# A graph layer with attention, mixing and experts: the PSUM banks and the places in the step of the chain of maxima

## The chip, the cores and the metric

The kernel runs on one core of a Trainium2 chip. The metric is the device time of one execution in microseconds; before the change it is 8320.49 us, the median of three runs (8315.88 to 8325.9). The core has five engines with a queue of instructions each, worked off in order: TensorE (PE, with its weight loads PEld), VectorE (DVE), ScalarE (ACT), GpSimd (POOL) and SyncE (SP). Results of PE go to PSUM, which here is used as eight banks of 512 float32 per partition.

## The reference

One block works on 6250 nodes of 256 features and 200,000 edges. The input is normalised; then come a graph network of three attention layers, a mixing layer of linear attention, and a mixture of eight experts, each added to the stream. What the change touches is the attention over edges, which for each layer is

```python
xh = (h @ W).reshape(n, heads, d)
a_s = (xh * att_src).sum(-1)
a_d = (xh * att_dst).sum(-1)
alpha = jax.nn.leaky_relu(a_s[src] + a_d[dst], NEG_SLOPE)
amax = jax.ops.segment_max(alpha, dst, num_segments=n)
e = jnp.exp(alpha - amax[dst])
z = jax.ops.segment_sum(e, dst, num_segments=n)
alpha = e / (z[dst] + 1e-16)
out = jax.ops.segment_sum(xh[src] * alpha[:, :, None], dst, num_segments=n)
```

Layers 0 and 1 have four heads, layer 2 has one. Every node also has an edge to itself.

## The kernel before, in words

The edges are ordered by their target. They are cut into rows of 128 edges, one edge on each partition, and each row belongs to one block of 128 target nodes. A **step** s has 32 rows; a layer has 51 steps, with one more for rare inputs. The loop in `sum_messages` runs over the steps, and inside it over 16 **iterations** i. In iteration i of step s the instructions of step s itself (its messages are summed) and of step n = s + 1 (its scores are made) are issued side by side. `Order.keep` fixes the order of the text for every engine, so an instruction's place in the loop is its place in its engine's queue.

What stands in the loop for step s:

- `gather`: POOL issues one indirect DMA for a row (L549), eight to a tile. The pool `rows` has 8, 9 and 7 tiles in layers 0, 1 and 2. A tile's gathers come after i = 3, 7, 11 and 15, when `pair` has read the tile that is to be overwritten.
- `hot` (L572, DVE) makes the matrices of zeros and ones that send an edge's message to its target; `weigh_step` multiplies the rows by the edges' weights, partly on ACT (L717) and partly on DVE (L710, which reads a copy of the weights in PSUM, `w_ps`, two of them in turn).
- `pair` (L747, PE): two rows are multiplied and summed in a bank of the pool `pm` (three banks). `add_up` (L760, DVE) adds the bank to the block's sum `acc` two iterations later; PE's pair i thus waits for DVE's add of pair i - 3.

And for step n:

- `scores` (L583, PE; L587, ACT), for two steps at once, in i = 2 to 6 of every second step.
- `spread` (L599, PE), four rows in each i from 0 to 7, sends the targets' scores to the edges; `load_lanes` (SP) and `compare_lanes` (L564, DVE) prepare it. L793 (DVE, i = 8) sums its three parts to `exs`.
- `row_scores` (L606, ACT, i = 2, 4, 6 and 9) copies the source scores out of the gathered rows to `asc`.
- `maxima`, a generator, makes the running maxima over edges of one target: transpose of asc on PE (L616, end of i = 9), scans on DVE (L620 to L625, top of 10), product on PE (L628, end of 10), scans over the rows (L632 to L641, top of 11), product (L644, end of 11), second scans (L652 to L665, top of 12), transpose back and two small products (L668, L671, L672, end of 12), the weights before exp (L676 to L689, top of 13), exp on ACT (L691, top of 14), copies and the column of maxima (L696, L700, DVE, end of 14).

All PSUM tiles of scores, spread and maxima have the name `sm` in a pool of two banks: a tile takes the bank that is free when its turn comes. Another bank, `lane_ps`, is written by DVE alone: it holds the lanes 0 to 127 and the two `w_ps`. With three banks for `pm` and two for the work beside, all eight are in use.

Beside the steps runs other work in pieces, `beside.step()` at the end of each iteration: the mixing layer in layer 0; and in every layer `Layer.update` for four finished blocks of nodes at a time (weights of the self edge L1450, L1453, norms, the next layer's projection, and in layer 2 the experts L1589 to L1606).

Of the kernel before, what the change touches and what calls it, by code (L numbers as in the profile page):

```python
# [7 lines left out]
F32 = mybir.dt.float32  # L8
# [7 lines left out]
P = 128  # L16
# [466 lines left out]
def sum_messages(tc, pools, consts, q, node_rows, adn, h, acc, beside, begin, slot, last,  # L483
# [92 lines left out]

    def scores(s):


        pt = smp.tile([P, 3 * h, SU], F32, name="sm")  # L580
        for i in range(4):
            for k in range(i * 3 * h // 4, (i + 1) * 3 * h // 4):
                nc.tensor.matmul(pt[:, k, :], adt[:, k // 3, k % 3, :], T[s]["block_hot"],  # L583
                                 start=True, stop=True)
            yield
        A[s] = wk.tile([P, h, 3, SU], BF16, name="adc")
        nc.scalar.copy(A[s].rearrange("p k j c -> p (k j) c"), pt)  # L587
# [5 lines left out]
    def spread(s, c0, n):  # L593

        m = M[s]
        if c0 == 0:
            m["ex"] = smp.tile([P, SU, h, 3], F32, name="sm")
        for c in range(c0, c0 + n):
            nc.tensor.matmul(m["ex"][:, c], lanes[s * subs + c // SUB][:, c % SUB, :],  # L599
                             adc(s)[:, :, :, c // 2], start=True, stop=True)  # L600

    def row_scores(s, k):
        m = M[s]
        if k == 0:
            m["asc"] = wk.tile([P, h, SU], F32, name="asc")
        nc.scalar.copy(m["asc"][:, :, k * SUB:(k + 1) * SUB].rearrange("p h c -> p c h"),  # L606
                       rows[s * subs + k][:, :, body:])

    def maxima(s):

        m, t = M[s], T[s]
        asc, exs = m["asc"], m["exs"]
        run = M[s - 1]["run"] if s else run0[:h]
        cut, joins = t["cut"][:hs], t["joins"]
        at = smp.tile([P, P], F32, name="sm")
# [11 lines left out]
        pe = smp.tile([P, 2, SU], F32, name="sm")  # L627
# [15 lines left out]
        pc = smp.tile([P, 2, SU], F32, name="sm")  # L643
# [3 lines left out]
        nc.vector.tensor_scalar(on[:h, :h], consts["ident"][:h, :h], run, None, op0=OP.mult)  # L647
        u = lp.tile([P, 2, h, SU], F32, name="u")
        nc.vector.tensor_add(u[:, 0], asc, exs)
        yield  # L650
# [16 lines left out]
        mt = m["mt"] = smp.tile([P, h, SU], F32, name="sm")  # L667
        nc.tensor.transpose(mt.rearrange("p h c -> p (h c)"), mx[:hs, :],  # L668
                            consts["ident"][:hs, :hs])
        po = smp.tile([P, 2, HEADS], F32, name="sm")  # L670
        nc.tensor.matmul(po[:, 0, :h], consts["ones"][:h, :], on[:h, :h], start=True, stop=True)  # L671
        nc.tensor.matmul(po[:, 1, :h], consts["ones"][:hs, :], new[:hs, :h], start=True,  # L672
                         stop=True)
        yield

        nc.vector.tensor_tensor(u[:, 1], mt, exs, op=OP.add)  # L676
# [17 lines left out]
        if half:  # L694
            m["w_ps"] = consts["w_ps"][:, s % 2].rearrange("p (h c) -> p h c", h=h)
            nc.vector.tensor_copy(m["w_ps"], w)  # L696
# [80 lines left out]
    for s in range(-1, end):  # L777
# [7 lines left out]
        for i in range(HSU):  # L785

            if made and i in (2, 4, 6, 9):
                row_scores(n, (2, 4, 6, 9).index(i))
            if made and 10 <= i <= 14:
                next(chain)  # L790
            if made and i == 8:
                M[n]["exs"] = wk.tile([P, h, SU], F32, name="exs")
                nc.vector.tensor_reduce(M[n]["exs"].rearrange("p k c -> p c k"), M[n]["ex"],  # L793
                                        axis=AX.X, op=OP.add)
            if s < 0 and i * GRP < NB:
                nc.vector.memset(acc[:, i * GRP:min(NB, (i + 1) * GRP), :], 0.0)
# [12 lines left out]
            if made and i == 9:  # L809
                chain = maxima(n)  # L810
            if made and 9 <= i <= 12 or made and i == 14:
                next(chain, None)

            if made and i < 8:
                spread(n, i * GRP, GRP)
                if i % 2:
                    load_lanes(n * subs + i // 2 + nlanes)
                    if i < 7:
                        compare_lanes(n * subs + i // 2 + 1)
            if made and i == HSU - 1:  # L820
                compare_lanes((n + 1) * subs)
            if 2 <= i <= 6:
                next(ahead, None)
# [399 lines left out]
def graph_block(ctx, tc, i, out):  # L1223
# [66 lines left out]
    for l, h in enumerate(heads):  # L1290
        W = C + 2 * h
        with ExitStack() as lc:
# [6 lines left out]
            ps = pool("lane_ps", 1, space=PS).tile([P, 3, P], F32, name="lane_ps")  # L1299
            consts["lane_ps"] = ps[:, 0]  # L1300
            nc.vector.tensor_copy(consts["lane_ps"], consts["lane"])
            consts["w_ps"] = ps[:, 1:]
            pmp, smp = pool("pm", 3, space=PS), pool("smp", 2, space=PS)
# [50 lines left out]
class Experts:  # L1354
# [26 lines left out]
class Layer:  # L1381
# [26 lines left out]
    def update(self, pools, where, stream, beside=None):  # L1408
# [41 lines left out]
        nc.vector.tensor_tensor(xv, xv, ws[:, 0, :n, :, None].to_broadcast([P, n, h, d]),  # L1450
# [3 lines left out]
                                ws[:, 1, :n, :, None].to_broadcast([P, n, h, d]), op=OP.mult)  # L1454
# [223 lines left out]
```

## Time and profile before

| what | value |
|---|---|
| median of three runs | 8320.49 us |
| the profiled execution | 8415.92 us |
| its span | 8414.1 us |
| mean granted clock of TensorE | 0.794 |
| PE busy | 5892.1 us, 70% |
| VectorE busy | 4682.9 us, 56% |
| ScalarE busy | 3410.1 us, 41% |
| GpSimd busy | 4829.7 us, 57% |
| gathers, L549 | 4896, 981 ns each |
| steps of layer 0 | 266 to 2785 us |
| steps of layer 1 | 2932 to 5367 us |
| steps of layer 2 | 5485 to 8243 us |

The first starts and last starts of L757, which comes once a step, give the three stretches. The profile is one execution; a line such as L628 is a line of the kernel before. In the groups, what stands behind the bar is the time for which the engine was idle just before these instructions, and what released it. "issue" means that nothing in the record ended just before, "remote" that the release was seen but not an instruction of the record that ended with it. The ends of matmuls are modelled.

### The profile page before, as it was taken

Reading aid. Unit: us, or ns where it says so; the run is one execution under the profiler, and the core shown is the slowest. Engines: PE = TensorE matmul, PEld = TensorE weight load, DVE = VectorE, ACT = ScalarE, POOL = GpSimd, SP = SyncE. Lnnn points to the kernel's source line nnn. Section 1 sums busy time; section 2 is a strip of 40 time slices with the busy share of each in tenths; the row PEclk is TensorE's granted clock in tenths of the full one; section 3 lists DMA queues with packets and bytes.
Section 4 is the critical chain, followed back from the end, with each engine's and each line's share of the span. In section 5 each row is a group of like instructions: output and inputs, shape, how many; then the busy total and the mean of one; then the engine's idle time right before and its main releaser. Section 6 shows DMA issues by size and latency. Waiting matters only on the chain. (4 is left out here: it accounts for less than half of the span.)

```text
span 8414.1 us, 98030 instructions
## 1 busy us (share of the span) xinstructions
PE 5892.1 (70%) x24601; PEld 4047.1 (48%) x24601; DVE 4682.9 (56%) x13248; ACT 3410.1 (41%) x10628; POOL 4829.7 (57%) x4942
## 2 busy tenths in 40 slices
PE   4577777766665356555566656458889888898998
PEld 3344455544443234434344444235666656566666
DVE  4456666666665455555556555445445445555552
ACT  2344544444443233433333344224444444444443
POOL 3565656565666466666666666456555555555550
PEclk8787877776767677776666776668999999999999
DMA  5444444444444344444444444334444444554452
GB/s 163 118 134 124 132 119 131 117 127 128 136 124 117 83 116 120 122 126 121 116 122 132 121 119 128 91 103 142 144 140 143 142 134 137 146 147 140 148 149 84
DMA packets 616289, 1070.08 MB, mean 127 GB/s; under 512 B 193175, under 2 KB 348167, under 8 KB 615706
## 3 DMA queue, kind: packets, MB, share of 16 engines
q0 software_dynamic: 236672, 661.50, 28.3%
q1 hardware_dynamic: 370590, 389.03, 15.3%
q10 hardware_dynamic: 8444, 13.02, 0.4%
q8 instruction: 214, 3.51, 0.2%
q14 instruction: 369, 3.02, 0.1%
HBM read 1008.69 MB, written 56.03 MB: 127 GB/s over the span
## 5 line engine op out<-in xcount | busy, mean ns | idle before, releaser
L549 POOL DMA_INDIRECT g<-node_rows,src_t x4896 | 4800.6, 981 | 3292.7 <-issue 1366.5
L747 PE MATMUL pm<-g,hot 128*128 128x264 f32 (+1 forms) x9792 | 3376.0, 482 | 1271.0 <-issue 584.3
L747 PEld LDWEIGHTS pm<-g,hot 128*128 128x128 f32 x9792 | 2148.3, 235 | 2020.3 <-issue 864.8
L717 ACT ACTIVATE g<-g,w 128x65 f32<-128x65 f32 (+1 forms) x8160 | 2382.6, 370 | 207.0 <-issue 191.9
L760 DVE TENSOR_TENSOR acc<-acc,pm 128x264 f32 (+1 forms) x2448 | 1030.5, 421 | 687.5 <-remote 278.3
L572 DVE TENSOR_TENSOR hot<-lane_ps,lane_t 128x1024 f32<-128x1024 f32 x612 | 744.2, 1216 | 0.0
L710 DVE TENSOR_TENSOR g<-g,lane_ps 128x520 f32<-128x520 f32 x816 | 559.5, 686 | 32.8 <-issue 31.0
L691 ACT ACTIVATE w<-w 128x128 f32<-128x128 f32 (+1 forms) x153 | 43.2, 282 | 1139.4 <-DVE u L456 500.4
L599 PEld LDWEIGHTS <-hot_t 128*128 128x128 bf16 x4896 | 323.0, 103 | 345.6 <-issue 146.4
L1594 ACT ACTIVATE moe_h<-fa,moe_b 128x512 f32<-128x512 f32 (+1 forms) x208 | 137.8, 662 | 758.8 <-PE fa L1589 460.5
L1589 PE MATMUL fa<-et,moe_w 128*128 128x512 f32 (+1 forms) x832 | 412.3, 621 | 45.3 <-DVE eo L1606 24.5
L1601 PE MATMUL fa<-moe_w,moe_h 128*128 128x256 f32 x1600 | 396.8, 390 | 36.7 <-ACT moe_h L1594 25.5
L1601 PE MATMUL fk<-moe_w,moe_h 128*128 128x256 f32 x1536 | 383.0, 393 | 26.5 <-DVE eo L1606 23.9
L1589 PE MATMUL fk<-et,moe_w 128*128 128x512 f32 (+1 forms) x832 | 384.5, 585 | 18.0 <-ACT moe_h L1594 10.2
L599 PE MATMUL sm<-adc,hot_t 128*128 128x12 bf16 (+1 forms) x4896 | 329.1, 179 | 74.0 <-issue 59.5
L793 DVE TENSOR_REDUCE exs<-sm 128x128 f32<-128x384 f32 (+1 forms) x153 | 69.4, 454 | 546.4 <-remote 386.0
L1601 PEld LDWEIGHTS fa<-moe_w,moe_h 128*128 128x128 f32 x1600 | 294.1, 191 | 90.6 <-ACT moe_h L1594 36.1
L1601 PEld LDWEIGHTS fk<-moe_w,moe_h 128*128 128x128 f32 x1536 | 289.9, 195 | 72.1 <-DVE eo L1606 27.8
L628 PE MATMUL sm<-ends,hcol 128*4 128x64 f32 (+1 forms) x306 | 47.8, 246 | 393.9 <-DVE ends L625 186.1
L1606 DVE SCALAR_TENSOR_TENSOR eo<-fa,share,eo 128x256 f32<-128x256 f32 x200 | 96.1, 481 | 408.6 <-PE fa L1601 239.5
L564 DVE TENSOR_SCALAR hot_t<-hot_t,pidx 128x1024 bf16<-128x1024 bf16 x612 | 299.3, 489 | 41.5 <-DMA hot_t<-q_lane_rows 34.9
L620 DVE TENSOR_TENSOR_SCAN mx_f<-cut_t,sm 128x128 f32<-128x128 bf16 (+1 forms) x153 | 63.2, 413 | 333.8 <-remote 250.7
(385 smaller groups left out, 5827.5 us busy)
## 6 DMA issues: line engine op xcount, KB each, us to landing
hot_t<-q_lane_rows SPq DMA_DIRECT2D x612, 256.0 KB
moe_w<-in_L_ffn_W_dram SPq DMA_DIRECT2D x208, 512.0 KB
g<-node_rows,src_t POOLq DMA_INDIRECT x4896
ea<-node_rows SPq DMA_DIRECT2D x24, 528.0 KB
et<-xnt SPq DMA_DIRECT2D x24, 512.0 KB
hid<-eo SPq DMA_DIRECT2D x24, 512.0 KB
eold<-hid SPq DMA_DIRECT2D x24, 512.0 KB
node_rows<-r ACTq DMA_DIRECT2D x12, 528.0 KB
```

What stands on the lines that cost most here:

```text
L549: nc.gpsimd.indirect_dma_start(out=t[:, c, :], out_offset=None, in_=node_rows, in_offset=bass.IndirectOffsetOnAxis(ap=T[s]["src"][:, i:i + ...
L564: nc.vector.tensor_scalar(lanes[m], lanes[m], consts["pidx"], None, op0=OP.is_equal)
L572: nc.vector.tensor_tensor(t, consts["lane_ps"][:, None, :].to_broadcast([P, SUB, P]), T[s]["lane"][:, k * SUB:(k + 1) * SUB, None].to_broa ...
L599: nc.tensor.matmul(m["ex"][:, c], lanes[s * subs + c // SUB][:, c % SUB, :], adc(s)[:, :, :, c // 2], start=True, stop=True)
L710: nc.vector.tensor_tensor(x, x, w[:, :, c:c + n].rearrange("p h c -> p c h")[:, :, :, None].to_broadcast([P, n, h, d1]), op=OP.mult)
L717: nc.scalar.activation(x, x, AF.Copy, scale=w[:, j, c + i:c + i + 1])
L747: nc.tensor.matmul(pm, m["hots"][2 * i // SUB][:, k + j, :], t[:, k + j, :], start=(j == 0), stop=(j == 1))
L760: nc.vector.tensor_tensor(at, at, pm, op=OP.add)
L1589: nc.tensor.matmul(pt[:, :w], w1[:, k, j * P:(j + 1) * P], xt[:, k, :w], start=(k == 0), stop=(k == 1))
L1594: nc.scalar.activation(hx[:, j, :w], pt[:, :w], AF.Gelu, bias=self.b1[:, e * 4 + j:e * 4 + j + 1])
L1601: nc.tensor.matmul(pt[:, :C], hx[:, j, t * P:(t + 1) * P], w2[:, j, :], start=(j == 0), stop=(j == 3))
L1606: nc.vector.scalar_tensor_tensor(y[:, t, :], pt[:, :C], share[:, t, e:e + 1], y[:, t, :], op0=OP.mult, op1=OP.add)
```

## The change

The pool of two banks becomes one bank with the name `sm` and one with the name `ex`. `spread` has `ex` for itself. `scores` takes the whole of `sm`, and `maxima` takes it once a step and lays its five results side by side in it. The places of the instructions in the step change with it, and the table gives them (top: before the iteration's weights and adds; end: after its pair).

| what | before | after |
|---|---|---|
| scores | i = 2 to 6 | i = 1 to 5 |
| row_scores | 2, 4, 6, 9 | 2, 4, 5, 7 |
| spread | 0 to 7, four each | 0 to 8, four, from i = 5 three |
| load_lanes | 1, 3, 5, 7 | 1, 3, 6, 8 |
| sum of spread (exs) | top of 8 | top of 11 |
| transpose of asc | end of 9 | end of 7 |
| first scans | top of 10 | end of 8 |
| product of the ends | end of 10 | top of 9 |
| scans over the rows | top of 11 | top of 10 |
| product back | end of 11 | end of 10 |
| second scans | top of 12 | end of 11 |
| transpose back, small products | end of 12, transpose first | top of 12, transpose last |
| weights, exp, copies | 13, 14, 14 | 13, 14, 14 |

`w_ps` becomes a single copy. `exs` is copied to the bank `lane_ps` for the first of its two sums. The weights of the self edge are written to that bank too and read from there.

```diff
+    def bank():
+        return smp.tile([P, 512], F32, name="sm")
...
-        pt = smp.tile([P, 3 * h, SU], F32, name="sm")
+        pt = bank()[:, :3 * hs].rearrange("p (k c) -> p k c", k=3 * h)
...
-            m["ex"] = smp.tile([P, SU, h, 3], F32, name="sm")
+            m["ex"] = smp.tile([P, SU, h, 3], F32, name="ex")
...
-        at = smp.tile([P, P], F32, name="sm")
+        sm = bank()
+        at = sm[:, :P]
...
-        pe = smp.tile([P, 2, SU], F32, name="sm")
+        pe = sm[:, P:P + 2 * SU].rearrange("p (k c) -> p k c", k=2)
...
-        pc = smp.tile([P, 2, SU], F32, name="sm")
+        pc = sm[:, P + 2 * SU:P + 4 * SU].rearrange("p (k c) -> p k c", k=2)
...
+        yield
         u = lp.tile([P, 2, h, SU], F32, name="u")
-        nc.vector.tensor_add(u[:, 0], asc, exs)
-        yield
+        exs_ps = consts["exs_ps"][:, :hs].rearrange("p (h c) -> p h c", h=h)
+        nc.vector.tensor_copy(exs_ps, m["exs"])
+        nc.vector.tensor_add(u[:, 0], asc, exs_ps)
...
-        mt = m["mt"] = smp.tile([P, h, SU], F32, name="sm")
-        nc.tensor.transpose(mt.rearrange("p h c -> p (h c)"), mx[:hs, :],
-                            consts["ident"][:hs, :hs])
-        po = smp.tile([P, 2, HEADS], F32, name="sm")
+        k = P + 4 * SU
+        po = sm[:, k + hs:k + hs + 2 * HEADS].rearrange("p (k h) -> p k h", k=2)
...
+        nc.tensor.transpose(sm[:, k:k + hs], mx[:hs, :], consts["ident"][:hs, :hs])
+        mt = m["mt"] = sm[:, k:k + hs].rearrange("p (h c) -> p h c", h=h)
...
-            if made and i in (2, 4, 6, 9):
-                row_scores(n, (2, 4, 6, 9).index(i))
-            if made and 10 <= i <= 14:
-                next(chain)
-            if made and i == 8:
+            if made and i in (2, 4, 5, 7):
+                row_scores(n, (2, 4, 5, 7).index(i))
+            if made and i == 11:
...
+            if made and i in (9, 10, 12, 13, 14):
+                next(chain)
...
-            if made and i == 9:
+            if made and i == 7:
                 chain = maxima(n)
-            if made and 9 <= i <= 12 or made and i == 14:
+            if made and i in (7, 8, 10, 11, 14):
                 next(chain, None)
...
-            if made and i < 8:
-                spread(n, i * GRP, GRP)
+            if made and i < 9:
+                spread(n, 4 * i - max(0, i - 5), 4 - i // 5)
...
-            if 2 <= i <= 6:
+            if 1 <= i <= 5:
                 next(ahead, None)
...
-            ps = pool("lane_ps", 1, space=PS).tile([P, 3, P], F32, name="lane_ps")
+            ps = pool("lane_ps", 1, space=PS).tile([P, 4, P], F32, name="lane_ps")
...
-            pmp, smp = pool("pm", 3, space=PS), pool("smp", 2, space=PS)
+            pmp, smp = pool("pm", 3, space=PS), pool("smp", 1, space=PS)
...
+        wp = consts["own_ps"][:, :2 * GRP * h].rearrange("p (k n h) -> p k n h", k=2, h=h)
         for k in range(2):
-            nc.vector.tensor_mul(ws[:, k, :n], ws[:, k, :n], rz[:, :n])
+            nc.vector.tensor_mul(wp[:, k, :n], ws[:, k, :n], rz[:, :n])
```

More of the change, by code (lines that the diff above doesn't have):

```diff
@@ L611, in maxima @@
         m, t = M[s], T[s]
-        asc, exs = m["asc"], m["exs"]
+        asc = m["asc"]
         run = M[s - 1]["run"] if s else run0[:h]
         cut, joins = t["cut"][:hs], t["joins"]
-        at = smp.tile([P, P], F32, name="sm")
+        sm = bank()
+        at = sm[:, :P]
         nc.tensor.transpose(at[:hs, :], asc.rearrange("p h c -> p (h c)"), consts["ident"])
@@ L673, in maxima @@
                          stop=True)
+        nc.tensor.transpose(sm[:, k:k + hs], mx[:hs, :], consts["ident"][:hs, :hs])
+        mt = m["mt"] = sm[:, k:k + hs].rearrange("p (h c) -> p h c", h=h)
         yield
-        nc.vector.tensor_tensor(u[:, 1], mt, exs, op=OP.add)
+        nc.vector.tensor_tensor(u[:, 1], mt, m["exs"], op=OP.add)
         leaky(nc, u, u)
@@ L694, in maxima @@
         if half:
-            m["w_ps"] = consts["w_ps"][:, s % 2].rearrange("p (h c) -> p h c", h=h)
+            m["w_ps"] = consts["w_ps"].rearrange("p (h c) -> p h c", h=h)
             nc.vector.tensor_copy(m["w_ps"], w)
@@ L808, in sum_messages @@
                 blocks(s + k // subs, k % subs) if s >= 0 or k == subs else None
-            if made and i == 9:
+            if made and i == 7:
                 chain = maxima(n)
-            if made and 9 <= i <= 12 or made and i == 14:
+            if made and i in (7, 8, 10, 11, 14):
                 next(chain, None)
-            if made and i < 8:
-                spread(n, i * GRP, GRP)
[L816 to L819, printed above, removed]
+            if made and i < 9:
+                spread(n, 4 * i - max(0, i - 5), 4 - i // 5)
+                if i in (1, 3, 6, 8):
+                    load_lanes(n * subs + (1, 3, 6, 8).index(i) + nlanes)
+                if i in (1, 3, 5):
+                    compare_lanes(n * subs + i // 2 + 1)
             if made and i == HSU - 1:
                 compare_lanes((n + 1) * subs)
-            if 2 <= i <= 6:
+            if 1 <= i <= 5:
                 next(ahead, None)
@@ L1298, in graph_block @@
             lp, gp, wk = pool("lay", 1), pool("rows", (8, 9, 7)[l]), pool("scores", 2)
-            ps = pool("lane_ps", 1, space=PS).tile([P, 3, P], F32, name="lane_ps")
-            consts["lane_ps"] = ps[:, 0]
+            ps = pool("lane_ps", 1, space=PS).tile([P, 4, P], F32, name="lane_ps")
+            consts["lane_ps"], consts["w_ps"], consts["exs_ps"] = [ps[:, k] for k in range(3)]
+            consts["own_ps"] = ps[:, 3, :2 * GRP * HEADS]
             nc.vector.tensor_copy(consts["lane_ps"], consts["lane"])
-            consts["w_ps"] = ps[:, 1:]
-            pmp, smp = pool("pm", 3, space=PS), pool("smp", 2, space=PS)
+            pmp, smp = pool("pm", 3, space=PS), pool("smp", 1, space=PS)
             ew, es, eps_ = pool("nodes", 1), pool("nodes_sm", 2), pool("nodes_ps", 1, space=PS)
@@ L1449, in update @@
         xv = x[:, :n, :body].rearrange("p n (h d) -> p n h d", h=h)[:, :, :, :d]
-        nc.vector.tensor_tensor(xv, xv, ws[:, 0, :n, :, None].to_broadcast([P, n, h, d]),
+        nc.vector.tensor_tensor(xv, xv, wp[:, 0, :n, :, None].to_broadcast([P, n, h, d]),
                                 op=OP.mult)
@@ L1453, in update @@
         nc.vector.tensor_tensor(ov, acc[:, :, :, :d],
-                                ws[:, 1, :n, :, None].to_broadcast([P, n, h, d]), op=OP.mult)
+                                wp[:, 1, :n, :, None].to_broadcast([P, n, h, d]), op=OP.mult)
         yield
```

## The prediction, made before the changed kernel was run

> **What bounds the kernel now.** I read the busy time by stretch first, with the stretches cut at the three layers (columns: stretch, length, busy time of PE, PE weight loads, DVE, ACT, POOL, granted TensorE clock, DMA share, GB/s).
>
> ```profile
> 266.00:2785.00 2519.00, 1755.10 (x7274) 1184.03 (x7273) 1622.77 (x4501) 1146.87 (x4060) 1535.41 (x1568) 0.77 0.44 125
> 2932.00:5367.00 2435.00, 1460.19 (x5890) 1002.86 (x5889) 1392.89 (x3752) 937.68 (x3661) 1533.99 (x1560) 0.71 0.43 120
> 5485.00:8243.00 2758.00, 2367.86 (x10077) 1640.73 (x10077) 1418.69 (x4235) 1182.94 (x2545) 1547.49 (x1576) 0.91 0.47 139
> ```
>
> Each row is one layer of 51 steps: layers 0, 1, 2. In layers 0 and 1 nothing is above 70%; PE is at 70 and 60%, at a clock of 0.77 and 0.71. In layer 2 PE is at 86% and 0.91: that layer is PE's. A step takes 2519/50 = 50.4, 48.7 and 55.2 us.
>
> Next, POOL in layer 1 (groups by line within the layer; after the bar: busy, mean ns, idle before and what ended it).
>
> ```profile
> L549 POOL DMA_INDIRECT g<-node_rows,src_t x1560 | 1534.0, 983 | 892.7 <-issue 412.6 <-PE pm L747 213.6 <-remote 122.4
> ```
>
> A gather takes 0.98 us and the timeline shows 0.305 us between two that wait for nothing: 32 x 1.288 = 41.2 us a step. This is the floor of layers 0 and 1; the rest of POOL's idle time waits for row buffers that PE has not given back. So PE and DVE, waiting for each other, set 50.4 and 48.7.
>
> Where they wait: PE's and DVE's groups of layer 1.
>
> ```profile
> L747 PE MATMUL pm<-g,hot 128*128 128x264 f32 x3206 | 1243.2, 532 | 696.8 <-issue 282.0 <-DVE acc L760 203.6 <-ACT g L717 104.2
> L628 PE MATMUL sm<-ends,hcol 128*4 128x64 f32 x100 | 16.6, 260 | 150.9 <-DVE ends L625 69.9 <-DVE mx_b L621 40.2 <-DVE ends L624 24.8
> L644 PE MATMUL sm<-cf,hrow 4*128 4x64 f32 x100 | 26.9, 358 | 21.9 <-DVE cf L641 13.3 <-DVE rb L636 3.0 <-PE pm L747 2.6
> L668 PE MATMUL sm<-ident,mx_b 128*128 128x128 f32 x50 | 20.1, 401 | 57.7 <-DVE mx_b L660 53.2 <-DVE mx_f L657 4.6
> ...
> L793 DVE TENSOR_REDUCE exs<-sm 128x128 f32<-128x384 f32 x50 | 27.9, 559 | 283.3 <-remote 260.6 <-PE pm L747 20.3 <-PE sm L599 2.3
> ```
>
> The chain of maxima (i = 9 to 14 of a step's 16 iterations) goes from PE to DVE and back four times, each answer wanted half an iteration later. L793 (i = 8) needs the spread matmuls that PE issued just before. "remote" there means that DVE was released well after the record has the matmul ended: PE is late by its own, and more freedom doesn't cure that part.
>
> The starts of L747 in the timeline, sorted by place in the step, give PE's idle time ahead of pair i in layers 0, 1 and 2: pair 9: 73, 189, 38; pair 14: 67, 167, 6 us. Pair 9 needs a bank that add L760 of pair 6 frees, and that add stands behind L793 on DVE. Pair 14 needs the add behind L676 to L689. In layer 1, pairs 8 to 14 take 26.3 us of a step, and the nine others 21.7.
>
> **The change, part by part.**
>
> *Banks and places.* The chain's idle time on PE, summed over the layers: pair 9 (held by L793) 300; L628 89.8 + 150.9 + 59.2 = 300; L644 66.6 + 21.9 + 38.6 = 127; pair 14 240: 967 us. After the change L793 is at i = 11 where spread ends at i = 8 (from one boundary to over two iterations); the transpose is at the end of i = 7 and its scans at the end of i = 8; L628 at the top of 9, its readers at the top of 10; L644 at the end of 10, its reader at the end of 11; the transpose back (L668) at the top of 12, its reader at the top of 13. Each round trip gains about one iteration (3 us). Against it: PE now has less lead where L628 and L668 wait (an iteration's top instead of its end), and L668 stands behind the two small products, 0.87 us later by the timeline. I take half of the 967 as PE's own lateness, and two thirds of the other half as gone: -320 us (ends: 0 and -880. The latter is what pairs 8 to 14 cost above the pace of the nine others: 4.9, 9.4 and 3.3 us a step in the three layers, times 50). L668's own 131 us stay; +20 for its lost lead (0 to +60).
>
> *One bank against a rule.* The transposes and products of the chain share a bank, and the Trainium skill, PSUM — Partial Sum Buffer, PSUM bank collisions raise a hardware error, wants accesses guarded by bank and quadrant, not by address: each PE write would wait for any DVE read of the bank. Four writes a step, each behind a scan (L657: 476 ns), would be 4 x 153 x 0.476 = 291 us. But in this chain each PE write takes what DVE computed after its last read of the bank, so the wait is there already (the row of L668 ends on mx_b, the scan itself); only scores, at i = 1, must wait for L700 at i = 14 before. I take 0.
>
> *row_scores from 9 to 7.* The fourth copy L606 now heads ACT's i = 7 and the transpose on PE follows it.
>
> ```profile
> L606 ACT COPY asc<-g 128x8 f32<-128x8 f32 x199 | 38.7, 194 | 103.3 <-DMA g<-node_rows,src_t 102.8
> ```
>
> This is layer 2: ACT there already waits for rows at the old place. The rows pool has 7 tiles in layer 2, so this tile's gathers are released by pair 3 of the same step, take 8 x 1.255 = 10 us on POOL, and land 1.9 us after the last issue (the shortest waits of L606). From the last gather's end to pair 7 the layer has a median of 1.0 us (lower quarter -1.0), to pair 9, 7.8. Landing plus a 0.2 us copy against the end of pair 7, step by step: PE would wait 1.8 us on average, 51 x 1.8 = +92 us on the engine that bounds the layer. Layers 0 and 1 (8 and 9 tiles) have 9.7 and 19.4 us: nothing. Below: 0, if PE is late anyway; above: +200, if ACT, held in order, also brings L717 and the gelu L1594 late (2 us more a step).
>
> *exs to PSUM.* One copy a step more, nearest row L696 (288 ns with four heads): 153 x 0.29 = +44 us on DVE, ahead of pick on its queue, where the matmul of the end of i = 10 is awaited anyway; exposed for a third: +15 (0 to +44). own_w written to PSUM: 78 small products of another destination, 0.
>
> *POOL's port.* By the Trainium skill, SBUF — State Buffer, Who interferes with whom, a DVE operation with two SBUF inputs blocks a GpSimd one that reads SBUF for its whole length: 78 x 1.16 (L1450, L1453) + 153 x 0.244 (L649) = 128 us of POOL would come free. The page infers that descriptor generation is not stopped so. The trace lies between: of all 4896 gathers (median 949 ns) what is above 945 ns and lies most beside L1450, L1453 and L649 sums to 11 + 8 + 2: 20 us. And POOL is not the bound (it waits 417 us beyond its pace in layer 1). I take 0 (to -20).
>
> *Queue of SP.* The lane loads of i = 5 and 7 come at 6 and 8, three tiles ahead: L564 waits 34.9 us for them in all; 0. Single w_ps: written at i = 14 after its last reader at 13, on one engine: 0.
>
> Sum: -320 + 20 + 92 + 15 = -193. The profiled execution took 8415.9 (span 8414.1), so 8223; the median of the runs, 8320.5, is 0.9887 of it: 8130. I say **8140 us**, -2.2%.
>
> **The rivals.**
>
> *Slower: layer 2 pays, layers 0 and 1 give nothing.* The waits of 0 and 1 are PE's own lateness ("remote", "issue", clock 0.71), so they only move, and layer 2 has 1.8 + 2.0 us a step of rows awaited (+194), less 50 of its own chain, plus 35: +179, so 8595 x 0.9887 = 8498. It decides as soon as layer 2's wait is above (320 - 35)/51 = 5.6 us a step, or above 1.8 with the gain under 127. For it: the 102.8 us at L606, PE at 86%. Against: half of PE's wait in 0 and 1 is released by DVE itself. 25%.
>
> *POOL's pace.* Layers 0 and 1 fall half the way to 41.2: (9.2 + 7.5)/2 x 50 = -418; 8416 - 418 + 20 = 8018, so 7927. For it: the clock rises with a busier PE (0.91 in layer 2), which shortens L747 (532 to 420 ns). Against: that PE's lateness must go too. 12%.
>
> *No change.* PE and DVE meet at the add L760 instead; what the chain gives, layer 2 takes: 8320. 8%.
>
> The forecast has 55%. A measurement of this kernel can tell 0.2% (17 us) from no change. Faster: all but the upper tail of the forecast's own range (8020 to 8290), and POOL's pace: 0.66; same 0.08; slower 0.26. The range that leaves out a fifth: 7960 to 8430; it holds part of the slower case.
>
> **What would show it.** Right: idle before L628 under 150 us and before pair 9 under 150; L793 with almost no wait; steps of layers 0 and 1 near 47.5 and 45.5; in layer 2 the transpose of asc (5.0 us idle now) with 50 to 150 us, released by L606, and L606 with over 150 us for rows. Wrong: layer 2 longer than 2850 us, or DVE's waits coming back in full at L760 in layers 0 and 1 with their granted clock no higher. L1450 and L1453 keep their length, and gathers beside them 949 ns.

## The result and the profile after

The changed kernel takes 8312.95 us, the median of 20 runs (8300.43 to 8352.71). The kernel before, in 20 runs beside it, takes 8277.64 us (8247.65 to 8325.9). The ratio is **1.0035, 95% interval 1.0022 to 1.0048**: by it 29 us slower (35 by the medians), where 8140 us were forecast.

The two profiles alone would mislead. The span fell from 8414.1 to 8312.1 us, but the profiled execution of before was a long one, 138 us above the median of its 20 runs. Another profile of the same kernel (below) has 8324.7 us. So in what follows I compare where the waits stand; the verdicts come from the ratios of many runs.

The lines of the changed kernel lie a little lower in the text: L747 is now L754, L760 is L767, L793 is L798, L606 is L610, L616 is L621, L620 is L625, L628 is L633, L634 is L639, L644 is L649, L668 is L679, L671 is L676, L672 is L677, L676 is L683. The kernels of the experiments have line numbers of their own again; there the names in a row (such as acc<-acc,pm for the add) tell which instruction it is.

First the busy time by layer (columns as in the prediction):

```profile
261.00:2771.00 2510.00, 1734.90 (x7276) 1188.49 (x7275) 1646.15 (x4552) 1143.25 (x4061) 1521.56 (x1568) 0.78 0.44 125
2913.00:5312.00 2399.00, 1447.49 (x5897) 1018.26 (x5893) 1417.66 (x3804) 941.26 (x3666) 1516.69 (x1560) 0.70 0.44 122
5418.00:8141.00 2723.00, 2363.65 (x10088) 1639.98 (x10089) 1433.52 (x4287) 1187.39 (x2549) 1532.21 (x1576) 0.92 0.48 141
```

A step takes 50.2, 48.0 and 54.5 us. PE is busy 69, 60 and 87% of the three layers, as before. The clock did not rise with it: 0.78, 0.70, 0.92.

Then PE's groups in layer 1, the ones that the prediction wanted shorter:

```profile
L754 PE MATMUL pm<-g,hot 128*128 128x264 f32 x3209 | 1234.6, 533 | 405.1 <-issue 190.8 <-DVE acc L767 120.2 <-remote 26.5
...
L649 PE MATMUL sm<-cf,hrow 4*128 4x64 f32 x100 | 29.7, 391 | 205.6 <-DVE cf L646 148.9 <-issue 36.9 <-DMA g<-node_rows,src_t 16.9
L677 PE MATMUL sm<-new,ones 128*128 128x4 f32 x100 | 27.1, 341 | 22.9 <-DVE new L672 17.2 <-issue 3.0 <-DVE mx_b L667 1.3
L676 PE MATMUL sm<-on,ones 4*128 4x4 f32 x100 | 26.4, 332 | 79.1 <-DVE mx_f L664 56.8 <-DVE pick L659 13.4 <-DVE carry L662 6.8
...
L633 PE MATMUL sm<-ends,hcol 128*4 128x64 f32 x100 | 17.2, 268 | 172.9 <-DVE ends L630 83.7 <-DVE mx_b L626 48.6 <-issue 33.3
L621 PE MATMUL sm<-ident,asc 128*128 128x128 f32 x50 | 15.0, 300 | 16.0 <-ACT asc L610 8.5 <-issue 7.5
```

Read the number after the second bar. The pair products wait 405 instead of 697 us, so pair 9 is indeed free (0 us of idle time ahead of it in all three layers, 189 before in this one). But the product back (L649) waits 206 instead of 22, the product of the ends (L633) 173 instead of 151. The sum over the chain and the pairs is 928 us before (697 + 151 + 22 + 58) and 902 after (405 + 206 + 173 + 79 + 23 + 16). **The waits moved from one instruction to the next.**

DVE, in the same layer, tells the same story from the other side; first before, then after:

```profile
L760 DVE TENSOR_TENSOR acc<-acc,pm 128x264 f32 x800 | 337.8, 422 | 269.3 <-remote 145.1 <-issue 42.8 <-PE sm L583 32.2
...
L620 DVE TENSOR_TENSOR_SCAN mx_f<-cut_t,sm 128x128 f32<-128x128 bf16 x50 | 20.9, 418 | 142.9 <-remote 123.0 <-issue 11.8 <-PE pm L747 7.3
...
L676 DVE TENSOR_TENSOR u<-sm,exs 128x128 f32<-128x128 f32 x50 | 14.1, 281 | 54.6 <-remote 34.3 <-issue 13.5 <-PE pm L747 5.2
...
L634 DVE TENSOR_TENSOR_SCAN rf<-joins_t,rf,sm 4x32 f32<-4x32 bf16 x50 | 13.5, 269 | 40.6 <-PE pm L747 21.3 <-remote 8.3 <-issue 5.5
```

```profile
L767 DVE TENSOR_TENSOR acc<-acc,pm 128x264 f32 x800 | 338.6, 423 | 336.0 <-remote 144.7 <-issue 75.8 <-PE ex L603 60.6
L798 DVE TENSOR_REDUCE exs<-ex 128x128 f32<-128x384 f32 x50 | 27.1, 542 | 0.2 <-issue 0.2
L625 DVE TENSOR_TENSOR_SCAN mx_f<-cut_t,sm 128x128 f32<-128x128 bf16 x50 | 21.0, 419 | 164.0 <-remote 146.4 <-PE ex L603 11.7 <-PE sm L621 4.5
...
L683 DVE TENSOR_TENSOR u<-sm,exs 128x128 f32<-128x128 f32 x50 | 14.2, 284 | 45.2 <-remote 16.1 <-PE sm L679 13.5 <-issue 11.1
L639 DVE TENSOR_TENSOR_SCAN rf<-joins_t,rf,sm 4x32 f32<-4x32 bf16 x50 | 13.5, 269 | 227.9 <-remote 214.8 <-issue 9.9 <-PE sm L633 1.2
```

The sum of the spread waited 283 us before and now 0.2. The scan over the rows (L639) waited 41 and now 228. Over these five lines the sum was 791 us before (L760 269, L793 283, L620 143, L676 55, L634 41) and is 773 after. The word to see is "remote": 522 us of the 773 after (mostly 145 + 146 + 215), and 571 us of the 791 before. PE's matmul has ended in the record, and DVE is released only later. How much later can be read from the starts and ends: the 24 "remote" waits of L639 end, in the median, 10.8 us after the recorded end of its matmul L633, and the 37 of L793 before ended 5.0 us after that of its last spread matmul. In all 61 cases DVE was released by a semaphore that only PE raises. As the ends of matmuls are modelled, PE may well have been at work where the record shows it idle. Whichever DVE instruction is the next to want an answer from PE seems to pay for this.

Layer 2, the transpose of asc, the product of the ends and the pairs, first before, then after, and then what the transpose waits for after:

```profile
L747 PE MATMUL pm<-g,hot 128*128 128x258 f32 x3202 | 932.2, 420 | 144.7 <-issue 108.5 <-ACT g L717 25.2 <-ACT p L1552 7.7
...
L616 PE MATMUL sm<-ident,asc 128*32 128x128 f32 x50 | 15.1, 303 | 5.0 <-issue 5.0
L628 PE MATMUL sm<-ends,hcol 32*1 32x64 f32 x100 | 14.4, 227 | 59.2 <-DVE ends L625 48.2 <-DVE mx_b L621 4.2 <-issue 4.1
```

```profile
L754 PE MATMUL pm<-g,hot 128*128 128x258 f32 x3208 | 935.7, 421 | 98.6 <-issue 83.6 <-DMA g<-node_rows,src_t 8.2 <-ACT g L724 3.4
...
L621 PE MATMUL sm<-ident,asc 128*32 128x128 f32 x50 | 15.8, 317 | 101.4 <-ACT asc L610 101.2
L633 PE MATMUL sm<-ends,hcol 32*1 32x64 f32 x100 | 14.9, 235 | 0.5 <-DVE ends L630 0.5
```

```profile
L610 ACT COPY asc<-g 128x8 f32<-128x8 f32 x200 | 39.3, 196 | 319.0 <-DMA g<-node_rows,src_t 318.9
```

PE waits 101 us for ScalarE's copy, which waits 319 us for gathered rows. The chain's other waits in this layer fell by about as much: L633 from 59 to 0.5, the pair products from 145 to 99.

### The profile page after: what moved, and what is told of

It is laid out like the page before. It is cut to its first block, busy times and chain, and to the rows that moved or that the text cites. A ratio compares the mean times of both kernels' runs of the same rounds, so it can differ in the third digit from the quotient of the medians.

```text
span 8312.1 us, 97980 instructions
## 1 busy us (share of the span) xinstructions
PE 5851.8 (70%) x24601; PEld 4063.7 (49%) x24601; DVE 4745.5 (57%) x13401; ACT 3411.9 (41%) x10628; POOL 4784.7 (58%) x4942
## 5 line engine op out<-in xcount | busy, mean ns | idle before, releaser
L754 PE MATMUL pm<-g,hot 128*128 128x264 f32 (+1 forms) x9792 | 3348.1, 481 | 868.0 <-issue 437.3
L754 PEld LDWEIGHTS pm<-g,hot 128*128 128x128 f32 x9792 | 2155.5, 235 | 1560.8 <-issue 690.6
L767 DVE TENSOR_TENSOR acc<-acc,pm 128x264 f32 (+1 forms) x2448 | 1031.3, 421 | 889.8 <-remote 305.3
L603 PEld LDWEIGHTS <-hot_t 128*128 128x128 bf16 x4896 | 356.3, 105 | 359.4 <-issue 155.6
L603 PE MATMUL ex<-adc,hot_t 128*128 128x12 bf16 (+1 forms) x4896 | 358.1, 179 | 71.8 <-issue 60.3
L610 ACT COPY asc<-g 128x32 f32<-128x32 f32 (+1 forms) x612 | 136.4, 223 | 526.0 <-DMA g<-node_rows,src_t 478.2
L649 PE MATMUL sm<-cf,hrow 4*128 4x64 f32 (+1 forms) x306 | 71.8, 321 | 334.1 <-DVE cf L646 200.5
L633 PE MATMUL sm<-ends,hcol 128*4 128x64 f32 (+1 forms) x306 | 49.2, 252 | 303.2 <-DVE ends L630 140.9
```

The source lines that it names most:

```text
L754: nc.tensor.matmul(pm, m["hots"][2 * i // SUB][:, k + j, :], t[:, k + j, :], start=(j == 0), stop=(j == 1))
L767: nc.vector.tensor_tensor(at, at, pm, op=OP.add)
```

## The experiments

A ratio is the kernel's runs over runs of the kernel before in the same group, on the same chip. Not all groups ran on the same chip, and that turned out to matter. The kernel before takes 8286 us in the first group and 8392 us in the third (one chip, two times), 8402 us in the fourth on another, but **7229 and 7233 us in the second and fifth**, which ran on a third chip. I call it the 7230 chip, and the first two the 8300 chips. The chip of the result above isn't on record; its 8278 us are like theirs. The letters of the theories in the quoted expectations hold within their group.

**First group, 8300 chip: the kernel before again, its banks, one move, and the ceiling of the chain.**

The kernel before, unchanged, for a second profile:

> The kernel before, unchanged, for a second profile. Its first profiled execution took 8415.9 us where 20 runs without have a median of 8277.6. Theory A (the change only moves waits): profile near 8280 to 8320, and the stretches of layers 0, 1 and 2 then lie at about 2490, 2400 and 2730 us, so that the three layers after the change (2510, 2399, 2723) are each within 1% of before. Theory B (layers 0 and 1 gained, layer 2 lost): layer 2 before is at 2650 us or less, layers 0 and 1 at 2520 and 2430.

One run, 8326.44 us; the layers take 2490, 2430 and 2705 us from the first pair of step 1 to that of step 51 (the first profile, read alike: 2519, 2435, 2758). Profiles of one kernel thus differ by up to 53 us in a layer, and a difference of that size between two profiles proves nothing.

Only the banks, everything at its old place:

```diff
-            m["ex"] = smp.tile([P, SU, h, 3], F32, name="sm")
+            m["ex"] = smp.tile([P, SU, h, 3], F32, name="ex")
...
-        at = smp.tile([P, P], F32, name="sm")
+        sm = bank()
+        at = sm[:, :P]
...
-            pmp, smp = pool("pm", 3, space=PS), pool("smp", 2, space=PS)
+            pmp, smp = pool("pm", 3, space=PS), pool("smp", 1, space=PS)
```

> The kernel before with the pool's two rotating banks replaced by one for spread and one for scores and the chain, every instruction at its old place. If sharing a bank adds waits of its own, slower by 0.3% or more; if, as the prediction said, each write already waits for the later read, the same within 0.2%.

8275.13 us, ratio 0.9991 (0.9973 to 1.0009). One bank for the whole chain costs nothing that can be measured, as the prediction had it.

The same, and of the places only that of the sum of the spread:

```diff
-            if made and i == 8:
+            if made and i == 11:
                 M[n]["exs"] = wk.tile([P, h, SU], F32, name="exs")
```

> The banks of e2, and of the moves only one: the sum of spread (exs) from i = 8 to i = 11; the chain of maxima and row_scores stay at their old places. Theory 1 (the wait at exs was real and the chain's new places gave the gain back): PE's 300 us ahead of pair 9 go, layer 2's transpose keeps 5 us, time 1 to 2% under before. Theory 2 (PE was late by itself, and the wait only moves to the next meeting of DVE and PE): the same within 0.3%, with the 300 us found again at the transpose's scans (L620) and at L628.

8266.91 us, ratio **0.9971** (0.9956 to 0.9987). PE's idle time ahead of pair 9 falls from 300 to 80 us in sum, and of these 220 us the kernel gains 24. Where the rest went shows on DVE over the whole span, with the banks alone:

```profile
L765 DVE TENSOR_TENSOR acc<-acc,pm 128x264 f32 (+1 forms) x2448 | 1029.5, 421 | 658.5 <-remote 293.1 <-PE pm L752 149.8 <-issue 64.4
...
L798 DVE TENSOR_REDUCE exs<-ex 128x128 f32<-128x384 f32 (+1 forms) x153 | 69.4, 454 | 496.3 <-remote 355.7 <-PE ex L603 80.5 <-PE pm L752 30.4
```

and with the move:

```profile
L765 DVE TENSOR_TENSOR acc<-acc,pm 128x264 f32 (+1 forms) x2448 | 1029.8, 421 | 1049.4 <-remote 472.5 <-PE pm L752 270.8 <-PE ex L603 86.2
...
L798 DVE TENSOR_REDUCE exs<-ex 128x128 f32<-128x384 f32 (+1 forms) x153 | 67.3, 440 | 0.0
```

The sum of the spread waits 496 us less and the adds 391 us more. PE's idle time ahead of all pairs together stays where it was (1252 and 1249 us).

The waits of the chain of maxima taken away: each engine reads a constant where the other's answer stood. The sum of the spread keeps its place and its wait.

```diff
+        at = consts["lane_ps"]
         f = lp.tile([P, P], F32, name="mx_f")
...
-        nc.tensor.matmul(pe[:h], hcol, ends[:hs], start=True, stop=True)
+        nc.tensor.matmul(pe[:h], hcol, consts["ident"][:hs, :2 * SU], start=True, stop=True)
+        pe = consts["lane_ps"][:, :2 * SU].rearrange("p (k c) -> p k c", k=2)
```

> The kernel before with the chain cut: every DVE and PE instruction of the maxima is kept, but PE multiplies constants and DVE reads constants in PSUM, so that neither waits for the other in the chain (the maxima and so the weights are not the reference's). It leaves the ceiling of any new placing. If the chain's round trips bound layers 0 and 1: over 6% faster, steps of layers 0 and 1 at 42 to 45 us. If those waits are PE's own lateness that only moves: under 2%, with the time found at the adds of pm and at exs.

8107.86 us, ratio **0.9807** (0.9786 to 0.9827). This is the ceiling for the maxima: their products and scans without any wait between PE and DVE are worth 1.9%, 160 us (143 to 177). In the prediction's 967 us it stands for L628, L644 and pair 14, 667 us of idle time. The 300 us of pair 9 are not in it: PE still waits 278 us there, and DVE 242 us at the sum of the spread in layer 1 alone. Their move is the run before this one; both together were not run. DVE and PE in layer 1 of this kernel, by group:

```profile
L765 DVE TENSOR_TENSOR acc<-acc,pm 128x264 f32 x798 | 337.3, 423 | 459.4 <-remote 294.2 <-issue 78.4 <-PE sm L599 23.9
```

```profile
L752 PE MATMUL pm<-g,hot 128*128 128x264 f32 x3200 | 1263.1, 539 | 743.9 <-issue 333.5 <-DVE acc L765 271.1 <-remote 28.9
```

With the waits of the maxima gone, the adds wait 459 us instead of 269 and the pair products 744 instead of 697. The layer still takes 2323 us, 46.5 a step, far from GpSimd's 41.2.

**Second group, 7230 chip: the parts on another chip.**

Only the work in VectorE's bank, on the kernel before (own weights, copy of exs, one `w_ps`):

```diff
-        nc.vector.tensor_add(u[:, 0], asc, exs)
+        exs_ps = consts["exs_ps"][:, :hs].rearrange("p (h c) -> p h c", h=h)
+        nc.vector.tensor_copy(exs_ps, exs)
+        nc.vector.tensor_add(u[:, 0], asc, exs_ps)
...
-            nc.vector.tensor_mul(ws[:, k, :n], ws[:, k, :n], rz[:, :n])
+            nc.vector.tensor_mul(wp[:, k, :n], ws[:, k, :n], rz[:, :n])
```

> The kernel before with only the third part of the change: the self edge's weights and a copy of exs written to the bank that DVE alone writes, one w_ps instead of two; banks and places as before. If POOL's blocked gathers (20 us by the trace) or the rule's 128 us reach the end: faster by 0.2% (rule: up to 1.5%). If POOL is not the bound and the copy (153 x 0.28 = 43 us of DVE) is half exposed: slower by 0.1 to 0.3%. I expect the same within 0.2%.

7194.92 us against 7229.23, ratio 0.9956 (0.9942 to 0.9969): a gain here, and more than the 0.2% expected at most.

The changed kernel with layer 2 at the old places (the order inside the chain stays that of the change):

```diff
-            if made and i in (2, 4, 5, 7):
-                row_scores(n, (2, 4, 5, 7).index(i))
+            if made and i in copies:
+                row_scores(n, copies.index(i))
...
+    copies = (2, 4, 5, 7) if h > 1 else (2, 4, 6, 9)
+    tops = (9, 10, 12, 13, 14) if h > 1 else (10, 11, 12, 13, 14)
+    ends = (7, 8, 10, 11, 14) if h > 1 else (9, 10, 11, 12, 14)
```

> The kernel after with layer 2 (one head) at the places of before, layers 0 and 1 as changed. If layer 2's wait for the gathered rows at the transpose is what the change lost (101 us of PE's idle time there after): 0.5 to 1% faster than after, so 0.2 to 0.6% faster than before, layer 2 at 2690 us or less. If PE makes that wait good elsewhere in the step: within 0.2% of after.

7204.52 us, ratio 0.9963 (0.9949 to 0.9977). The new places in layers 0 and 1 add nothing that these intervals show to what the bank part gives alone (0.9956).

The changed kernel with eight instead of seven row tiles in layer 2:

```diff
-            lp, gp, wk = pool("lay", 1), pool("rows", (8, 9, 7)[l]), pool("scores", 2)
+            lp, gp, wk = pool("lay", 1), pool("rows", (8, 9, 8)[l]), pool("scores", 2)
```

> The kernel after with 8 row tiles in layer 2 instead of 7, so that the gathers of the fourth tile start four iterations earlier. The transpose's wait in layer 2 (101 us) falls under 20 us. If this wait was on the path: as e6 or better (layer 2 at 2690 or less, 0.3 to 0.6% under before). If only the wait's place was wrong: as after.

7143.47 us, ratio **0.9889** (0.9874 to 0.9904), the best version on this chip. Layer 2 takes 2401 us against 2469 in the run with its old places: there PE waits 72 us for the transpose of asc even at the old place, and with the eighth tile 44 at the new one.

The kernel before with one of the two products of a pair left out:

```diff
-        for j in range(2):
-            nc.tensor.matmul(pm, m["hots"][2 * i // SUB][:, k + j, :], t[:, k + j, :],
-                             start=(j == 0), stop=(j == 1))
+        nc.tensor.matmul(pm, m["hots"][2 * i // SUB][:, k + 1, :], t[:, k + 1, :], start=True,
+                         stop=True)
```

> The kernel before with one of the two products of each pair left out (every other edge row is not summed), so PE has 4896 fewer matmul passes of 264 columns; all else, DVE's adds and the waits of the chain included, is kept. If layers 0 and 1 are bound by PE's own execution, which the record shows as DVE's 'remote' waits: their steps fall from 50 and 48.5 to 43 to 45 us, near POOL's 41.2, and the remote waits shrink by more than half. If they are bound by the round trips between PE and DVE: 47 us or more.

6992.31 us, ratio 0.9671 (0.9656 to 0.9686). Half of the instructions of PE's largest group are gone, and a step of layers 0 and 1 still takes 41.8 and 41.3 us (42.2 and 40.9 in the bank part's run); only layer 2 falls, from 49.3 to 45.4. On this chip layers 0 and 1 go at the 41.2 us that the prediction worked out for GpSimd, and layer 2 is PE's. The expectation was written for steps of 50 us; on an 8300 chip this kernel was not run, so that it doesn't test PE's lateness there.

**Third group, 8300 chip: what adds to what.**

The changed kernel once more:

> The changed kernel once more, to stand beside the others of this call on one chip. Theory A (what the change does depends on what the chip lets bound layers 0 and 1): where the kernel before takes near 7230 us, the ratio is 0.995 to 0.998, because the part in VectorE's bank frees GpSimd and the wait for rows in layer 2 eats a part of it; where it takes near 8290 us, 1.002 to 1.005 as measured. Theory B (the chain's new places cost time everywhere): over 1.002 on either. In both, TensorE waits 80 to 130 us in layer 2 at the transpose of the source scores.

8419.63 us against 8391.9, ratio 1.0033 (1.0012 to 1.0054): the first result again. In layer 2 the transpose waits 99 us.

The sum of the spread moved, once more:

> Two banks in turn by name, and the sum of the spread moved from the top of i = 8 to the top of i = 11, everything else at its old place. It gave 0.9971 where the kernel before takes 8286 us. Theory A (the gain is TensorE's freedom at pair 9, which counts where TensorE is late): there 0.995 to 0.999 again; where the kernel before takes 7230 us and layers 0 and 1 go at GpSimd's pace, 0.998 to 1.001. Theory B (it is worth the same everywhere): 0.996 to 0.998 on either.

8356.91 us, ratio **0.9958** (0.9945 to 0.9971): faster than the kernel before for the second time, and faster than the changed kernel beside it.

The kernel before with the eighth row tile:

> The kernel before with 8 instead of 7 tiles of gathered rows in layer 2, nothing else. Theory A (layer 2 waits for rows even before the change): 0.990 to 0.995 where the kernel before takes 7230 us (60 us of layer 2, as in the pair of the changed kernel with and without), and 0.995 to 1.000 where it takes 8290 us, since ScalarE waited 103 us for rows there with TensorE busy meanwhile. Theory B (the eighth tile only takes back what the earlier copy costs): within 0.2% on either.

8395.69 us, ratio 1.0007 (0.9993 to 1.002). Nothing, though ScalarE's wait at L606 in layer 2 falls from 103 to 15 us. On the 7230 chip the two runs with seven and with eight tiles (7204.52 and 7143.47) lie 61 us apart, though they differ in the places of layer 2 as well.

The sum of the spread at i = 11, the bank part and the eighth tile together:

> The parts that gained by themselves: bank by name, the sum of the spread at i = 11, the self edge's weights and the copy for VectorE in the bank it alone writes, 8 row tiles in layer 2; the chain of maxima and the copies of source scores at their old places. Theory A (the parts act on different resources and add): 0.985 to 0.990 where the kernel before takes 7230 us, 0.992 to 0.998 where it takes 8290 us, in both below the changed kernel of this call. Theory B (the changed kernel's places are needed for it): not below the changed kernel.

8399.69 us, ratio 1.0016 (1.0002 to 1.0031). A miss: expected was 0.992 to 0.998. If the parts multiply, the bank part costs half a per cent here: 1.0016 / (0.9958 x 1.0007) = 1.0051. GpSimd's gathers, over the whole span, show what became of the relief: first in the run with the sum's move alone, then in this one (which has the eighth tile too).

```profile
L549 POOL DMA_INDIRECT g<-node_rows,src_t x4896 | 4806.1, 982 | 3220.4 <-issue 1347.1 <-PE pm L752 421.4 <-PE ex L603 300.1
```

```profile
L549 POOL DMA_INDIRECT g<-node_rows,src_t x4896 | 4748.2, 970 | 3317.3 <-issue 1342.8 <-PE pm L754 552.2 <-remote 307.4
```

A gather became 12 ns shorter, 58 us in all, and GpSimd waits 97 us longer; the wait that grew most is the one for PE's pair products to give rows back (421 to 552). Here what was freed on an engine that waits was only waited longer.

**Fourth group, another 8300 chip: the parts out of the changed kernel.**

Own weights left in SBUF:

```diff
-        wp = consts["own_ps"][:, :2 * GRP * h].rearrange("p (k n h) -> p k n h", k=2, h=h)
+        wp = ws
```

> The changed kernel with the self edge's weights left in SBUF as before (L1450 and L1453 of the kernel before read two SBUF inputs again); the rest of the change stays. Theory A (own weights in VectorE's bank free GpSimd, whose earlier gathers cost TensorE time where TensorE is late): 0.997 to 1.000 where the kernel before takes over 8200 us, and 0.998 to 1.001 where it takes 7230 us; the gathers' mean goes back from 969 to 978 ns or more. Theory B (the copy of exs costs): 1.002 to 1.005. Theory C (the places cost): 1.002 to 1.005.

8399.67 us against 8401.74, ratio 0.9998 (0.998 to 1.0015): what theory A expected.

The copy of exs left out:

```diff
-        exs_ps = consts["exs_ps"][:, :hs].rearrange("p (h c) -> p h c", h=h)
-        nc.vector.tensor_copy(exs_ps, m["exs"])
-        nc.vector.tensor_add(u[:, 0], asc, exs_ps)
+        nc.vector.tensor_add(u[:, 0], asc, m["exs"])
```

> The changed kernel without the copy of exs to VectorE's bank (its first sum reads exs from SBUF as before); the rest stays. It takes 153 copies of 0.28 us off VectorE. Theory B (the copy costs, as it stands on the chain's way): 0.997 to 1.001 where the kernel before takes over 8200 us. Theory A (own weights) and theory C (places): 1.002 to 1.005.

8391.32 us, ratio 0.9988 (0.9973 to 1.0004): what theory B expected, so that neither part alone carries the loss.

Both of these edits, and two `w_ps` in turn again, so that only the banks and the places remain:

> The changed kernel without anything in VectorE's bank: own weights and exs in SBUF, two copies of the weights in turn; only banks by name and the new places. Theory C (the places cost): 1.002 to 1.005 where the kernel before takes over 8200 us. Theories A and B (VectorE's bank costs): 0.996 to 0.999, since the sum of the spread is at i = 11 here too, and it gained 0.3 to 0.4%; less what layer 2 waits for rows.

8395.51 us, ratio **0.9988** (0.9973 to 1.0003). All the places together give 10 us, which is not clear of nothing. The sum of the spread alone gave 24 and 35 us, in other groups; the intervals overlap, so that the chain's new places took some of it back is likely, not shown.

Only the bank part on the kernel before, the kernel of the second group:

> The kernel before with only the work in VectorE's bank (own weights, copy of exs, one copy of the weights instead of two), banks and places as before. It gave 0.9956 where the kernel before takes 7229 us. Theories A and B: 1.003 to 1.007 where it takes over 8200 us. Theory C: 0.999 to 1.001 there. Where it takes 7229 us: 0.994 to 0.997 again.

8454.88 us, ratio **1.0051** (1.0029 to 1.0072). The same edit that gains 0.44% on the 7230 chip loses 0.51% here. Places and bank part multiply to 0.9988 x 1.0051 = 1.0039, within the intervals of the changed kernel (1.0033 and 1.0035), which itself did not run in this group. The loss is the bank part's; that the places cost 0.2% or more is refuted on this chip.

**Fifth group, meant to split the bank part; it came to the 7230 chip.**

The copy of exs alone:

```diff
-        nc.vector.tensor_add(u[:, 0], asc, exs)
+        exs_ps = consts["exs_ps"][:, :hs].rearrange("p (h c) -> p h c", h=h)
+        nc.vector.tensor_copy(exs_ps, exs)
+        nc.vector.tensor_add(u[:, 0], asc, exs_ps)
```

> The kernel before with only the copy of exs to VectorE's bank and the first sum reading it there. 153 copies of 0.28 us are 43 us. Theory B (the copy stands on the path in full): 1.004 to 1.006 where the kernel before takes over 8200 us. Theory A (own weights, through earlier gathers): 0.999 to 1.001. Where the kernel before takes 7230 us: theory A and B 1.000 to 1.002, with the gathers beside it shorter.

7228.77 us against 7232.52, ratio 0.9994 (0.9987 to 1.0001).

The own weights alone:

```diff
-            nc.vector.tensor_mul(ws[:, k, :n], ws[:, k, :n], rz[:, :n])
+            nc.vector.tensor_mul(wp[:, k, :n], ws[:, k, :n], rz[:, :n])
```

> The kernel before with only the self edge's weights in VectorE's bank. It adds no instruction. Theory B: 0.999 to 1.001 where the kernel before takes over 8200 us, since it only frees GpSimd, which is not the bound there. Theory A: 1.003 to 1.006. Where the kernel before takes 7230 us: 0.995 to 0.998, since GpSimd's pace is the bound there.

7207.75 us, ratio 0.9958 (0.9945 to 0.9972). On this chip the whole gain of the bank part (0.9956) is that of the own weights; the copy is free. For the 8300 chips the split stays **open**: against the changed kernel's 1.0033 and 1.0035 of other groups, each of the two taken out gave some 0.4% back, both together (with the two `w_ps`) no more, and neither was run alone there. So the loss shows only where both stand, and why is not known.

How the chips differ shows in layer 1 of the copy's run (busy time by engine, then groups of PE, ACT and DVE), beside the rows of before in the prediction:

```profile
2433.00:4500.00 2067.00, 1360.16 (x5888) 908.14 (x5888) 1395.55 (x3802) 919.57 (x3662) 1567.25 (x1588) 0.75 0.52 144
```

```profile
L749 PE MATMUL pm<-g,hot 128*128 128x264 f32 x3200 | 1158.6, 500 | 376.8 <-ACT g L719 196.4 <-DVE acc L762 128.1 <-issue 41.7
```

```profile
L606 ACT COPY asc<-g 128x32 f32<-128x32 f32 x200 | 48.3, 241 | 798.1 <-DMA g<-node_rows,src_t 798.0
```

and the same row of the kernel before on the 8300 chip:

```profile
L606 ACT COPY asc<-g 128x32 f32<-128x32 f32 x198 | 46.1, 233 | 13.4 <-issue 11.6 <-DMA g<-node_rows,src_t 1.4
```

DVE again in the copy's run:

```profile
L762 DVE TENSOR_TENSOR acc<-acc,pm 128x264 f32 x798 | 335.8, 421 | 7.7 <-PE pm L749 1.5 <-issue 0.7
L795 DVE TENSOR_REDUCE exs<-sm 128x128 f32<-128x384 f32 x50 | 27.9, 557 | 44.9 <-PE sm L599 44.9
```

"remote" is no longer among the first releasers. The add waits 8 us instead of 269 and the sum of the spread 45 instead of 283; where it waits it starts 0.04 us after the recorded end of its last matmul. Now it is rows that are awaited: ScalarE waits 798 us for them (13 on the 8300 chip). By these waits PE is the late one on one chip, GpSimd on the other.

## Why the prediction was wrong

It said 8140 us, -2.2%; measured is +0.35%. By its own steps:

- **Chain of maxima, -320 us: this step failed.** It took the 967 us for which the record shows PE idle, put half of them down to PE's own lateness without a figure for the half, and booked two thirds of the rest as time gained. With the +20 and +92 of the same edits it forecast -208 us for places and banks. These alone gave 0.9988, 10 us (between 22 gained and 2 lost, by 8300 us). The maxima with all their waits removed gave 160 us of 667, and the sum of the spread at i = 11 gave 24 and 35 us of the 300 ahead of pair 9. The share of lateness was too small: in the five DVE rows of layer 1, 571 of 791 us are "remote" (260.6 of 283.3 at L793, the wait that was to go first). And what is taken away at one place comes back at the next: 496 us less at the sum of the spread were 391 us more at the adds. The idle times ahead of instructions that wait for the same late engine did not add up.
- **What the signs showed.** Idle time ahead of pair 9: 0, right. L793 without a wait: right. Idle time before L628 under 150: wrong, 277 us (104, 173, 0.5). Steps of layers 0 and 1 of 47.5 and 45.5 us: wrong, 50.2 and 48.0. Waits back at L760: part of them, in layer 1 269 to 336 us, most of the rest at L639. Gathers beside the products with the own weights at 949 ns, and these products as long as before: right (below).
- **Layer 2's rows, +92 us: right in place and size** as a wait (101 us at L621, ScalarE 319). It did not come on top in full: the other waits of the layer fell by 105 us (L633 59, the pair products 46). An eighth tile, which removes the wait for rows, gives nothing on the 8300 chip when put on the kernel before.
- **By layer, over the traces of the 8300 chips** (first to last start of the instruction L757, which comes once a step): layer 1 takes 2388 to 2412 us in the five traces with the new places and 2393 to 2410 in the three that move only the sum of the spread (one has the bank part and the eighth tile too), against 2425 to 2455 in the five with neither (the run without the waits of the maxima left aside). So its gain seems to be that of the sum alone, and the moved chain adds none. Layer 2, in the third and fourth group, takes 2779 to 2796 us with the new places and 2738 to 2771 without. So layer 2 probably paid some 20 to 30 us. The single differences lie within the 53 us by which two profiles can differ; that the sets do not overlap is what speaks for them.
- **Copy of exs +15, own weights 0, GpSimd's port 0 to -20: mis-sized.** The three terms are the bank part, measured at 1.0051: +42 us (24 to 60, by 8300 us). With the 10 us of the places this makes +32, and the result has +29. The upper end given for the copy was +44; the split was not settled. On GpSimd's side the sum of 20 us from the trace was too small: the gathers' mean fell from 981 to 971 ns, 45 us over 4896 (35 from the second profile of before, 58 between the two runs of the third group). The prediction's 128 us, worked out from the Trainium skill, SBUF — State Buffer, Who interferes with whom, were too high by a factor of two to four. The traces show when the page's rule, that a DVE operation with two SBUF inputs contends with a GpSimd instruction that reads SBUF, costs time. Of the gathers beside L1450 and L1453, the 44 that were already running when the operation began took 943 to 952 ns. The 53 that began while it ran took 1392 ns in the median and up to 1907, the longer the more of it was left, 23 us in all. After the change, the 52 that began beside L1459 or L1462 took 945 to 952. So an operation costs what is left of it when a gather begins, and not its whole length each time; and the page's inference that descriptor generation is spared does not fit gathers issued like this. The rest of the 45 us is not explained. As GpSimd was not the bound here, neither figure reached the end; on the 7230 chip the own weights gave 30 us.
- **One bank 0: right** (0.9991, at the old places). SP's queue and the single copy of the weights weren't tried alone.
- **The base.** The sum started at a profile 138 us over the median of the 20 runs, and its factor 0.9887 was taken from three runs. This adds noise, but no sign.
- **The rivals.** "No change", with 8%, came nearest in time (8320). The slower rival had the right sign and half of its mechanism, layers 0 and 1 giving next to nothing; but layer 2 did not pay 179 us. POOL's pace is what the 7230 chip shows, at the same kernel, and no edit brought the 8300 chips there. That PE's lateness only moves, which the slower rival and the prediction's own remark on "remote" had named, is what the runs bear out.

That the changed kernel as it stands would gain on the 7230 chip is likely from its parts (0.9963 with layer 2 at the old places, 0.9889 with eight tiles), but it wasn't run there.

## What to carry to other kernels

Before adding up idle times of a chain that two engines hand to and fro, run it once with the waits replaced by constants: it gives the ceiling of these waits (here 160 us, where their idle times summed to 667), and it costs one run. If most of a wait ends well after the producer's end in the record, expect that moving the consumer hands most of the wait to the next one, as here (220 us of idle time gone, 24 us gained). And what an edit is worth that relieves an engine can change its sign between chips: the same one gained 0.44% where GpSimd set the pace and lost 0.51% where PE was late, and why it lost is open.

## What the runs showed of the hardware that was not expected

The same kernel takes 7230 us on one chip and 8280 to 8400 us on two others, 14 to 16% apart. In the traces (on the 7230 chip that of the run with the copy) the three layers take 6653 us against 7712. The busy time of PE in them differs much less, 5307 us against 5583, and the granted clock is 0.81, 0.75 and 0.94 against 0.77, 0.71 and 0.91. By the record the larger part lies in idle time: in layer 1 the sum of the spread, where it waited, started 4.1 us (median) after the recorded end of its last matmul on the one and 0.04 us on the other. Why PE is late on these chips no run shows.

One kernel on one chip also moved between groups: the kernel before had a median of 8286 us in the first and 8392 us in the third. Only ratios within a group could carry the differences of 0.3% that this study is about.
